# Half blocks of 128 rows for the experts' last rows, in both layers of a two-layer network

## The chip, the core and the metric

One core of a Trainium2 chip. The core has five engines that run their own queues of instructions and wait for each other by semaphores: TensorE (PE in the profile; PEld is its loading of weights), VectorE (DVE), ScalarE (ACT), GpSimdE (POOL) and SyncE (SP, which here only starts transfers). The metric is the device time of one execution in microseconds (us), lower is better; times of a kernel are medians over several executions.

## The reference

4096 tokens of 256 channels pass through two layers. Each layer normalizes the tokens and adds an attention part and a part of experts to them, both computed from the same normalized tokens. Layer 0 has a state-space mixer and 16 experts of width 128, of which a router gives 4 to each token (plus two shared ones that take every token); layer 1 has a linear attention and 8 experts of width 512, of which each token gets 2. First the experts of layer 0, then those of layer 1:

```python
scores = jax.nn.sigmoid(x @ w_gate.T)
...
_, idx = jax.lax.top_k(masked, TOPK)
w = jnp.take_along_axis(scores, idx, axis=1)
w = w / (w.sum(-1, keepdims=True) + 1e-06) * ROUTE_SCALE
...
g = jax.nn.silu(jnp.einsum('th,efh->tef', x, w1_e))
u = jnp.einsum('th,efh->tef', x, w3_e)
routed = jnp.einsum('tef,ehf,te->th', g * u, w2_e, combine)
...
topk_scores, topk_idx = jax.lax.top_k(scores, k)
topk_probs = jax.nn.softmax(topk_scores, axis=-1)
h1 = jnp.einsum('bsd,efd->bsef', x, W1)
h2 = jnp.einsum('bsd,efd->bsef', x, W2)
hidden = jax.nn.silu(h1) * h2
expert_out = jnp.einsum('bsef,edf->bsed', hidden, W3)
```

The kernel doesn't compute every expert for every token as the formulas do. It sends each token's row only to the experts that were chosen for it: 4096 x 4 = 16384 rows in layer 0, 4096 x 2 = 8192 in layer 1. How many rows an expert gets is known only while the kernel runs.

## The kernel before, in words

**Blocks.** The rows of an expert are laid out in DRAM (`xg0_d`, `xg1_d`) in blocks of `RB` = 256 rows, `RPB` = 2 tiles of 128. Every expert starts a new block, so its last block is mostly not full; what is empty holds zeros and the numbers of spare tokens (`blanks`, L318, called by `fills`, L1027). At most `NB0` = 79 and `NB1` = 39 blocks can be needed. The program runs `FIRST0` = 72 and `FIRST1` = 36 of them in any case, and the others only under a guard that compares the count of blocks, `used`, with that (L1134 and L1135, L1545). A block that no expert needs runs on blank rows.

**Routing.** `places` (L224 to L290) works on DVE, on all 128 partitions alike. It counts the rows of each expert (`plb`, a sum over token tiles), compares the counts with multiples of 256 (L260) and sums the comparisons to blocks per expert (`n_b`, L262), sums these along the experts by one small addition after the other (L264 to L267), and from that makes the place of each token's row (`dest`), the expert of each block (`own`, `owner`: a comparison of all blocks with all experts, L285 to L288) and `used`. It is a generator: at each `yield` other work is put between. In layer 0 three pieces of the routing go into each of the first steps of the mixer's main loop; in layer 1 one piece goes beside each step of the attention's projections (`beside`, L1296). Then each token's row is scattered by POOL to its places (`dispatch0`, L678, from step `FILLED` = 14 of the main loop on; L1274 in layer 1, two scatters a step).

**Layer 0's blocks.** The main loop of the mixer has 128 steps. When the dispatch is done, ticks of the blocks go into the remaining steps, two per step as long as there are more ticks left than steps, then one; there are `FIRST0` + 3 = 75 ticks, and consecutive blocks are in different stages of a tick: `block_in` (L727, 4 transposes), `block_hidden` (L742, 4 matmuls of 256 columns, two records each in the trace, L749), `block_out` (L759, 2 matmuls, L766) and `block_add` (L774, 2 indirect transfers by POOL that add the rows to `moe_d`, L779, each behind those of the block before). SP loads the block's rows, its expert's weights and the rows' shares (`block_rows`, `block_weights`). The orders of POOL and SP are written out by hand; those of PE, DVE and ACT come from the scheduler that builds the program.

**Layer 1's blocks** run at the end with nothing beside them. `some1` (L1525) goes through them with the next block's transposes and the block before's output between the two halves of the hidden layer: `load1` (L1436: the owner's number is read into a register of SP, then weights of 1 MB, rows, and 0.5 MB of output weights), `turn1` (L1449), `hidden1` (L1473, 16 matmuls of 256 columns, 32 records, L1482), `output1` (L1490, 8 matmuls, 16 records, L1496; then the scaling by the share on ACT, L1500, and two indirect adds to `out`, L1504). The weights of the hidden layer have two buffers, so those of a block are loaded when the block two before has read its own. The rows have two buffers as well.

Of the kernel before, what the change touches and what calls it, by code (L numbers as in the profile page):

```python
# [18 lines left out]
P = 128  # L19
# [31 lines left out]
NB0 = T * TOPK0 // RB + E0 - 1  # L51
NB1 = T * TOPK1 // RB + E1 - 1
FIRST0 = T * TOPK0 // RB + E0 // 2
FIRST1 = T * TOPK1 // RB + E1 // 2
# [48 lines left out]
def two_layer_kernel(  # L103
# [47 lines left out]

    xg0_d = dram.tile([NB0 * RB, RW0], FP, name="xg0_d")
    xg1_d = dram.tile([NB1 * RB, RW1], FP, name="xg1_d")
# [42 lines left out]

    def expert_of(owner, b, ne, behind=True):

        (ins,), (e,) = nc.values_load_multi_w_load_instructions(
            owner[0:1, b : b + 1], (mybir.EngineType.SP,), min_val=0, max_val=ne - 1,  # L200
            bass_reorder=False,
        )
        if loads and behind:
            tc.add_manual_dep(
                ins.ins, loads[-1].ins.name,
                mybir.DependencyInfo(mybir.DependencyClass.NoSync, mybir.DependencyReason.DATA),
                reason="in the order of the blocks",
            )
        return e
# [14 lines left out]
    def places(wk, psum, rk, ne, k, nb, dest, own, owner, used=None):  # L224

        t3 = lambda n: wk.tile([P, NT, ne], FP, tag="pl" + n, name="pl" + n, bufs=1)
# [31 lines left out]
        nc.vector.tensor_tensor(c3, last(a[:, NT - 1, :], steps), mid(full, ne), ALU.is_gt)  # L260
        n_b = wk.tile([P, ne], FP, tag="n_b", name="n_b", bufs=1)
        nc.vector.tensor_reduce(n_b, c3, AX.X, ALU.add)  # L262
        upb = wk.tile([P, ne], FP, tag="upb", name="upb", bufs=1)
        nc.vector.tensor_copy(upb[:, 0:1], n_b[:, 0:1])  # L264
        for e in range(1, ne):
            nc.vector.tensor_tensor(
                upb[:, e : e + 1], upb[:, e - 1 : e], n_b[:, e : e + 1], ALU.add  # L267
            )
        if used is not None:
            nc.vector.tensor_copy(used, upb[:, ne - 1 : ne])  # L270
# [3 lines left out]
        nc.vector.tensor_tensor(n_b, upb, n_b, ALU.subtract)  # L274
        nc.vector.tensor_scalar(n_b, n_b, float(RB), None, ALU.mult)
        nc.vector.tensor_tensor(a, a, mid(n_b, NT), ALU.add)
# [9 lines left out]
        nc.vector.tensor_reduce(own, cmp, AX.X, ALU.add)  # L286
# [26 lines left out]
    own0 = wpool.tile([P, NB0], FP, name="own0")  # L313
    owner0 = wpool.tile([P, NB0], I32, name="owner0")
# [3 lines left out]
    def blanks(xg, n, rw, b0, b1):  # L318
        v = xg.rearrange("(b j p) c -> p b j c", j=RPB, p=P)
        for j in range(RPB):  # L320
            nc.sync.dma_start(v[:, b0:b1, j, :], mid(blank[:, j, :rw], b1 - b0))
# [22 lines left out]
    with tc.tile_pool(name="m", bufs=1) as mp, tc.tile_pool(  # L344
# [333 lines left out]
        def dispatch0():  # L678

            def load(i):  # L680
                if i < NT:
                    xs = moe.tile([P, RPB * DM], FP, tag="ys", name=f"xs0_{i}", bufs=3)[:, :RW0]
                    o = i % TPB * P
                    nc.sync.dma_start(xs[:, :DM], xn_d[0][i // TPB][o : o + P, :])
                    ahead.append(xs)

            ahead = []
            load(0)
            yield
            for i in range(NT):  # L690
                load(i + 1)
                xs = ahead.pop(0)
                nc.gpsimd.tensor_copy(xs[:, DM:], tail0[:, i, :])
                for k in range(TOPK0):
                    nc.gpsimd.indirect_dma_start(
                        out=views0[i * TOPK0 + k],
                        out_offset=bass.IndirectOffsetOnAxis(ap=dest0[:, i, k : k + 1], axis=0),
                        in_=xs,
                        in_offset=None,
                        bounds_check=NB0 * RB - 1,  # L700
                    )
                    yield
# [3 lines left out]
        def block_rows(m):  # L706
            xg = moe.tile([P, RPB, RW], FP, tag="xg", name=f"xg0_{m}", bufs=2)
            nc.sync.dma_start(
                xg, xg0_d[m * RB : (m + 1) * RB, :RW].rearrange("(j p) c -> p j c", p=P)
            )  # L710
            rows0[m] = xg

        def block_weights(m):
            e = expert_of(owner0, m, E0, False)
# [6 lines left out]
                ws, xg0_d[m * RB : (m + 1) * RB, RW:]  # L721
# [5 lines left out]
        def block_in(m):  # L727

            xg = rows0.pop(m)
            pt = psum(f"ptx0_{m}").rearrange("p (k t) -> p k t", k=KD)  # L730
            for k in range(KD):
                for j in range(RPB):
                    nc.tensor.transpose(
                        pt[:, k, j * P : (j + 1) * P], xg[:, j, k * P : (k + 1) * P], ident
                    )
            xgt = moe.tile([P, KD, RB], FP, tag="xgt", name=f"xgt0_{m}", bufs=2)
            nc.scalar.copy(xgt, pt)
            ids = moe.tile([P, RPB], I32, tag="ids", name=f"ids0_{m}", bufs=5)
            nc.scalar.copy(ids, xg[:, :, DM])
            act0[m] = xgt, ids  # L740

        def block_hidden(m):  # L742
            xgt, ids = act0.pop(m)
            w, ws = weights0.pop(m)
            pgu = psum(f"pgu0_{m}").rearrange("p (a t) -> p a t", a=2)
            for a in range(2):
                for k in range(KD):
                    o = (a * KD + k) * P
                    nc.tensor.matmul(  # L749
                        pgu[:, a, :], w[:, o : o + P], xgt[:, k, :],  # L750
# [3 lines left out]
            nc.scalar.activation(sl, pgu[:, 0, :], AF.Silu)  # L754
            hid = moe.tile([P, RB], FP, tag="hid", name=f"hid0_{m}", bufs=2)
            nc.vector.tensor_tensor(hid, sl, pgu[:, 1, :], ALU.mult)
            hid0[m] = w, hid, ws, ids

        def block_out(m):  # L759
            w, hid, ws, ids = hid0.pop(m)  # L760
            po = psum(f"po0_{m}").rearrange("p (j d) -> p j d", j=RPB)
# [3 lines left out]
            for j in range(RPB):  # L765
# [4 lines left out]
            for j in range(RPB):  # L770
                nc.scalar.activation(ys[:, j, :], po[:, j, :], AF.Copy, scale=ws[:, j : j + 1])
            ys0[m] = ys, ids

        def block_add(m):  # L774
            ys, ids = ys0.pop(m)
            parts = []
            for j in range(RPB):
# [12 lines left out]

        def blocks(at):

            for m in range(FIRST0 + 3):
                if at == 0:
                    if m == 0:
                        block_rows(0)
                        block_rows(1)
                        block_weights(0)
                    if m < FIRST0:
                        block_in(m)  # L800
                if at == 1 and 0 <= m - 1 < FIRST0:
                    block_hidden(m - 1)
                if at == 3 and m >= 3:
                    block_add(m - 3)
                if at == 2:
                    if 0 <= m - 2 < FIRST0:
                        block_out(m - 2)
                    if m + 1 < FIRST0:
                        block_weights(m + 1)
                    if m + 2 < FIRST0:  # L810
                        block_rows(m + 2)
# [215 lines left out]
        def fills():  # L1027

            for b in range(0, NB0, 6):
                blanks(xg0_d, NB0, RW0, b, min(b + 6, NB0))  # L1030
# [7 lines left out]
            for b in range(0, NB1, 4):  # L1038
                blanks(xg1_d, NB1, RW1, b, min(b + 4, NB1))
# [5 lines left out]
        moe, sends, ticks, todo, done = None, None, None, FIRST0 + 3, object()  # L1045
# [88 lines left out]
        n0 = nc.values_load(used0[0:1, 0:1], min_val=T * TOPK0 // RB, max_val=NB0)  # L1134
# [108 lines left out]
    own = big.tile([P, NB1], FP, name="own")  # L1243
    owner = big.tile([P, NB1], I32, name="owner")
# [3 lines left out]
    def route1():  # L1248
# [15 lines left out]
        for g in range(NFB):  # L1264
# [6 lines left out]
            for j in range(TPB):  # L1271
                i = g * TPB + j
                for k in range(TOPK1):
# [5 lines left out]
                        bounds_check=NB1 * RB - 1,  # L1279
# [156 lines left out]
    def load1(b):  # L1436
# [3 lines left out]
        nc.sync.dma_start(w, wv_[:, : 2 * KD * fd])  # L1440
        xg = wk.tile([P, RPB, RW1], FP, tag="xs", name=f"xg{b}")
        loads.append(nc.sync.dma_start(
            xg, xg1_d[b * RB : (b + 1) * RB, :].rearrange("(j p) c -> p j c", p=P)
# [5 lines left out]
    def turn1(b):  # L1449
        w, xg, w2 = rows1.pop(b)  # L1450
        wt = wk.tile([P, RPB, E1], FP, tag="wt", name=f"wt{b}", bufs=4)
        tc.keep_in_program_order(nc.vector.scalar_tensor_tensor(
            wt, mid(lane[:, :E1], RPB), own[:, b : b + 1], xg[:, :, RW:], ALU.is_equal, ALU.mult
        ))
        ws = wk.tile([P, RPB], FP, tag="ws", name=f"ws{b}", bufs=4)
        nc.vector.tensor_reduce(ws, wt, AX.X, ALU.add)
        ids = wk.tile([P, RPB], I32, tag="ids", name=f"ids{b}", bufs=5)
        tc.keep_in_program_order(nc.vector.tensor_copy(ids, xg[:, :, DM]))
        pt = trp.tile([P, KD, RB], FP, tag="tr", name=f"ptx{b}")
        for k in range(KD):  # L1460
            for j in range(RPB):
# [6 lines left out]
        nc.scalar.copy(xgt, pt)  # L1468
# [4 lines left out]
    def hidden1(b, f0):  # L1473
        w, xgt, hid = act1[b]
        nm = f"1_{b}_{f0}"
        pg = ps.tile([P, 2, RB], FP, tag="pg", name="pg" + nm)
        pu = ps.tile([P, 2, RB], FP, tag="pu", name="pu" + nm)
        for a, pt in enumerate((pg, pu)):
            for f in range(2):
                for k in range(KD):  # L1480
                    o = (a * KD + k) * fd + (f0 + f) * P
                    nc.tensor.matmul(  # L1482
                        pt[:, f, :], w[:, o : o + P], xgt[:, k, :],
# [3 lines left out]
        nc.scalar.activation(sl, pg, AF.Silu)  # L1487
        nc.vector.tensor_tensor(hid[:, f0 : f0 + 2, :], sl, pu, ALU.mult)  # L1488

    def output1(b):  # L1490
        w2, hid, ws, ids = out1.pop(b)
        po = ps.tile([P, RPB, DM], FP, tag="po", name=f"po1_{b}")
        ys = wk.tile([P, RPB, DM], FP, tag="ys", name=f"ys{b}", bufs=4)
        for j in range(RPB):
# [7 lines left out]
        for j in range(RPB):  # L1502
# [15 lines left out]
    def count():  # L1518
# [3 lines left out]
        n = nc.values_load(now[0:1, 0:1], min_val=T * TOPK1 // RB, max_val=NB1)  # L1522
        counted.append(n)

    def some1(b0, b1):  # L1525
        load1(b0)
        turn1(b0)
        if b0 + 1 < b1:
            load1(b0 + 1)
        for b in range(b0, b1):  # L1530
# [3 lines left out]
            if b > b0:  # L1534
                output1(b - 1)
            if b + 1 < b1:
                turn1(b + 1)
            hidden1(b, 2)
            if b + 2 < b1:
                load1(b + 2)  # L1540
        output1(b1 - 1)


    some1(0, FIRST1)
    with tc.If(counted[0] > FIRST1):  # L1545
        some1(FIRST1, NB1)
# [65 lines left out]
```

## Time and profile before

| | us |
|---|---|
| median of 3 runs (lowest to highest) | 2320.83 (2318.41 to 2330.72) |
| the profiled execution: its time | 2315.34 |
| the profiled execution: its span, first to last instruction | 2313.6 |
| from the start to the end of the mixer with layer 0's experts beside it | about 0 to 1645 |
| of it: layer 0's routing pieces until `dest` is there | until 245 |
| of it: rows scattered to the blocks | 283 to 931 |
| of it: blocks of layer 0 | about 930 to 1630 |
| shared experts, attention and routing of layer 1 | about 1645 to 1912 |
| blocks of layer 1 | 1912 to 2313.6 |

A row of the profile names an engine, a line of the kernel, an operation with what it writes and reads, its partitions x elements, and how often it occurred; then its busy time, the mean of one in ns, and the idle time of the engine just before it, with what ended most of that. A matmul's time is the time from its start to its modelled end, and matmuls are pipelined: how far their starts are apart is read from the timeline, which merges like instructions into one line (start, length, engine, line, what, how many). The mean granted TensorE clock of the execution was 0.977 of the full one.

### The profile page before, as it was taken

How to read it: one execution, taken by the hardware profiler on the slowest of the kernel's cores; microseconds unless marked ns; L12 is line 12 of the kernel's file. 1: busy time of each engine (PE TensorE's matmuls, PEld its weight loads, DVE VectorE, ACT ScalarE, POOL GpSimd, SP SyncE). 2: the span in 40 equal slices, each digit the busy share in tenths (PEclk: the TensorE clock that was granted, in tenths of full speed). 3: DMA queues.
4: the chain of work that ended last, by engine and by line, in shares of the span. 5: the costliest groups of instructions: out<-in, count | busy, mean ns of one | idle time of the engine just before them, and what ended most of it. 6: DMA issues, size and time to landing. Idle time of an engine off the chain costs nothing. (4 is left out here: it accounts for less than half of the span.)

```text
span 2313.6 us, 36420 instructions
## 1 busy us (share of the span) xinstructions
PE 2143.8 (93%) x12572; PEld 1699.5 (73%) x12572; DVE 1455.9 (63%) x3350; ACT 910.0 (39%) x1872; POOL 1466.7 (63%) x1280
## 2 busy tenths in 40 slices
PE   6787999999999989899998999999799989999998
PEld 5565777777777767777787878888465568888886
DVE  5799988888888878556565567778257441111111
ACT  5632344343333334344443444444134742222221
POOL 0345699888889889677887787887541652232232
PEclk9899999999999999999999999999899999999999
DMA  9577678644444444576777776665541356777774
GB/s 312 172 217 230 187 239 256 193 142 155 146 135 159 146 137 145 166 186 174 180 183 179 181 183 162 172 173 150 175 136 46 131 191 182 207 187 197 202 190 113
DMA packets 240605, 405.72 MB, mean 175 GB/s; under 512 B 39201, under 2 KB 178977, under 8 KB 235809
## 3 DMA queue, kind: packets, MB, share of 16 engines
q1 hardware_dynamic: 193424, 342.62, 46.5%
q0 software_dynamic: 40320, 55.21, 13.5%
q10 hardware_dynamic: 6672, 5.51, 0.7%
q8 instruction: 103, 1.69, 0.3%
q14 instruction: 86, 0.70, 0.1%
HBM read 288.57 MB, written 114.69 MB: 174 GB/s over the span
## 5 line engine op out<-in xcount | busy, mean ns | idle before, releaser
L375 DVE SCALAR_TENSOR_TENSOR cv<-pj,cw,cv 128x256 f32<-128x256 f32 x864 | 404.1, 480 | 104.4 <-ACT cv L373 95.4
L519 POOL TENSOR_TENSOR mm<-mm,btok 128x512 f32<-128x512 f32 x256 | 336.9, 1397 | 13.6 <-DVE mm L470 12.8
L470 DVE TENSOR_TENSOR_SCAN mm<-mm,eyes 128x256 f32<-128x256 f32 x512 | 319.0, 672 | 24.4 <-ACT eyes L476 24.4
L365 PE MATMUL pj<-xt,w_in 128*128 128x259 f32 (+1 forms) x1152 | 314.4, 398 | 10.2 <-DVE pj L361 6.8
L435 PE MATMUL pg<-xt,w_in 128*128 128x256 f32 x1024 | 277.8, 393 | 35.0 <-ACT gate L442 32.3
L1504 POOL DMA_INDIRECT out<-ys,ids x72 | 111.3, 1546 | 300.2 <-ACT ys L1500 267.1
L365 PEld LDWEIGHTS pj<-xt,w_in 128*128 128x128 f32 x1152 | 217.7, 195 | 78.3 <-issue 34.7
L779 POOL DMA_INDIRECT moe_d<-ys,ids x144 | 226.8, 1575 | 69.4 <-issue 23.3
L597 PE MATMUL po<-w_o,g 128*128 128x256 f32 x1024 | 256.3, 383 | 1.8 <-POOL g L1021 1.8
L435 PEld LDWEIGHTS pg<-xt,w_in 128*128 128x128 f32 x1024 | 187.0, 194 | 92.5 <-ACT gate L442 42.4
L1488 DVE TENSOR_TENSOR hid<-silu,pu 128x512 f32<-128x512 f32 x72 | 49.5, 688 | 321.6 <-PE pu L1482 321.6
L373 ACT ACTIVATE cv<-pj,cw 128x256 f32<-128x256 f32 x288 | 135.7, 472 | 240.8 <-PE pj L365 239.6
L509 POOL TENSOR_TENSOR hd<-hdt,dec 128x512 f32<-128x512 f32 x124 | 140.9, 1137 | 117.0 <-DVE hdt L500 112.9
L597 PEld LDWEIGHTS po<-w_o,g 128*128 128x128 f32 x1024 | 190.4, 191 | 29.1 <-issue 2.7
L1021 POOL TENSOR_TENSOR g<-g,gate 128x512 f32<-128x512 f32 x128 | 176.2, 1377 | 51.2 <-DVE g L574 29.2
L386 ACT ACTIVATE hc<-cv,bw 128x256 f32<-128x256 f32 x256 | 129.5, 507 | 164.4 <-DVE cv L375 164.1
L574 DVE SCALAR_TENSOR_TENSOR g<-hc,ch,py 128x128 f32<-128x128 f32 x512 | 144.9, 344 | 27.2 <-PE py L563 27.0
L589 ACT ACTIVATE g<-g 128x512 f32<-128x512 f32 x128 | 80.8, 632 | 202.1 <-POOL g L593 146.2
L474 DVE TENSOR_TENSOR cs<-cs,eyes 128x512 f32<-128x512 f32 x248 | 159.9, 675 | 0.0
L563 PE MATMUL py<-cs,state 128*64 128x128 f32 x1984 | 144.0, 284 | 14.2 <-issue 10.9
L563 PEld LDWEIGHTS py<-cs,state 128*64 128x64 f32 x1984 | 110.0, 139 | 59.5 <-issue 53.7
L749 PE MATMUL pgu<-xgt,w 128*128 128x256 f32 x576 | 142.8, 393 | 11.2 <-DVE state L545 11.1
(245 smaller groups left out, 3999.7 us busy)
## 6 DMA issues: line engine op xcount, KB each, us to landing
mm<-step_d SPq DMA_DIRECT2D x128, 512.0 KB, 4.5
cs<-from_d SPq DMA_DIRECT2D x124, 512.0 KB, 5.9
w<-in_w_ffn SPq DMA_DIRECT2D x36, 1024.0 KB, 5.7
w<-in_w_ffn SPq DMA_DIRECT2D x72, 384.0 KB, 3.2
xg_d<-blank SPq DMA_DIRECT2D x26, 828.0 KB, 8.4
xg<-xg_d SPq DMA_DIRECT2D x72, 260.0 KB, 4.1
w<-in_w_ffn SPq DMA_DIRECT2D x36, 512.0 KB, 6.5
xg_d<-blank SPq DMA_DIRECT2D x18, 536.0 KB, 8.4
```

The lines of the kernel that those rows point to most:

```text
L365: nc.tensor.matmul(pj[:, h0 : TB + HALO], w_in[:, k, INTER + c * P : INTER + (c + 1) * P], xts[b][:, k, h0 : TB + HALO], start=(k == 0), s ...
L375: nc.vector.scalar_tensor_tensor(cv, pj[:, i : i + TB], cw[:, c, i : i + 1], cv, ALU.mult, ALU.add)
L435: nc.tensor.matmul(pj[:, :TB], w_in[:, k, c * P : (c + 1) * P], xts[b][:, k, HALO:], start=(k == 0), stop=(k == KD - 1),)
L470: nc.vector.tensor_tensor_scan(m, m, eye, 0.0, ALU.mult, ALU.add)
L474: nc.vector.tensor_tensor(m, m, mid(c_in[:, j, :], QH), ALU.mult)
L519: nc.gpsimd.tensor_tensor(m, m, mid(blk["gm"][j], QH), ALU.mult)
L563: nc.tensor.matmul(py[(h % 2) * HP : (h % 2 + 1) * HP, h // 2, :], left[:, h, :], right[:, h, :], start=(a == 0 and h < 2), stop=(a == len ...
L574: nc.vector.scalar_tensor_tensor(g[:, i, :], hc[i][:, sl], d_ch[:, k : k + 1], py[:, i, :], ALU.mult, ALU.add,)
L597: nc.tensor.matmul(po[:, j, :], g[:, i, :], w_o[:, k, :], start=(k == 0 and j == 0), stop=(k == NCI - 1), skip_group_check=True,)
L749: nc.tensor.matmul(pgu[:, a, :], w[:, o : o + P], xgt[:, k, :], start=(k == 0), stop=(k == KD - 1),)
L779: nc.gpsimd.indirect_dma_start(out=moe_d[:, :], out_offset=bass.IndirectOffsetOnAxis(ap=ids[:, j : j + 1], axis=0), in_=ys[:, j, :], in_of ...
L1021: nc.gpsimd.tensor_tensor(gs[k], gs[k], gates[n][:, :, j * P : (j + 1) * P], ALU.mult)
```

## The change

Both layers get blocks of two sizes. An expert whose rows, counted modulo 256, leave a rest of 1 to 128 gives this rest to a half block of 128 rows instead of a whole block. There are 8 half blocks in layer 0 and 4 in layer 1 (`NH0`, `NH1`); if more experts have such a rest, the further ones take a whole block as before. The half blocks lie behind the whole ones in DRAM (`place`), and the program runs 64 and 32 whole blocks (`FIRST0`, `FIRST1`) and all half blocks unguarded, in the order of `mixed`: one half after every eight whole ones. The number of blocks that run stays 72 and 36. At most `NB0` = 71 and `NB1` = 35 whole blocks can be needed; those above 64 and 32 run under the guard, which compares with the count of whole blocks. In `places` a second comparison with the multiples of 256 plus 128 tells experts with such a rest from the others, two scans make the running sums in place of the chain of additions, rows of the rest get another place, the half blocks get their owners, and one more `yield` stands in it. Every operation of a block works on `nj` tiles of 128 rows, 2 or 1; the weights are loaded whole for each.

```diff
+def most(n, ne, nh):
+    return max(
+        (n - h - (ne - h) * (RB // 2 + 1)) // RB + ne - h + max(h - nh, 0) for h in range(ne + 1)
+    )
+
+NH0, NH1 = E0 // 2, E1 // 2
+NB0, NB1 = most(T * TOPK0, E0, NH0), most(T * TOPK1, E1, NH1)
+FIRST0, FIRST1 = T * TOPK0 // RB, T * TOPK1 // RB
...
+    def place(b, nb):
+        return (b * RB, RPB) if b < nb else (nb * RB + (b - nb) * P, 1)
+
+    def mixed(first, nb, nh):
+        n = first // nh
+        return [b for h in range(nh) for b in (*range(h * n, (h + 1) * n), nb + h)]
...
-        nc.vector.tensor_tensor(c3, last(a[:, NT - 1, :], steps), mid(full, ne), ALU.is_gt)
+        nc.vector.tensor_tensor(c3, last(n_e, steps), mid(full, ne), ALU.is_gt)
+        nc.vector.tensor_reduce(odd, c3, AX.X, ALU.add)
+        nc.vector.tensor_scalar_add(full, full, float(P))
+        nc.vector.tensor_tensor(c3, last(n_e, steps), mid(full, ne), ALU.is_gt)
         nc.vector.tensor_reduce(n_b, c3, AX.X, ALU.add)
-        nc.vector.tensor_copy(upb[:, 0:1], n_b[:, 0:1])
-        for e in range(1, ne):
-            nc.vector.tensor_tensor(
-                upb[:, e : e + 1], upb[:, e - 1 : e], n_b[:, e : e + 1], ALU.add
-            )
...
+        nc.vector.tensor_tensor(odd, odd, n_b, ALU.subtract)
+        nc.vector.tensor_tensor_scan(upo, ones[:, :ne], odd, 0.0, ALU.mult, ALU.add)
+        nc.vector.scalar_tensor_tensor(odd, upo, float(nh), odd, ALU.is_gt, ALU.mult)
+        nc.vector.tensor_tensor(n_b, n_b, odd, ALU.add)
+        nc.vector.tensor_tensor_scan(upb, ones[:, :ne], n_b, 0.0, ALU.mult, ALU.add)
+        nc.vector.tensor_copy(used, upb[:, ne - 1 : ne])
 
         yield
         nc.vector.tensor_tensor(a, a, w, ALU.add)
-        nc.vector.tensor_tensor(n_b, upb, n_b, ALU.subtract)
+        first, extra = s1("first"), s1("extra")
+        nc.vector.tensor_tensor(first, upb, n_b, ALU.subtract)
+        nc.vector.tensor_scalar(first, first, float(RB), None, ALU.mult)
+        nc.vector.tensor_scalar(
+            extra, upo, float(P), float(nb * RB - P), ALU.mult, ALU.add
+        )
+        nc.vector.scalar_tensor_tensor(extra, upb, -float(RB), extra, ALU.mult, ALU.add)
         nc.vector.tensor_scalar(n_b, n_b, float(RB), None, ALU.mult)
-        nc.vector.tensor_tensor(a, a, mid(n_b, NT), ALU.add)
+        nc.vector.tensor_tensor(b, a, mid(n_b, NT), ALU.is_ge)
+        nc.vector.tensor_tensor(b, b, mid(extra, NT), ALU.mult)
+        yield
+        nc.vector.tensor_tensor(a, a, mid(first, NT), ALU.add)
+        nc.vector.tensor_tensor(a, a, b, ALU.add)
         yield
...
-        nc.vector.tensor_reduce(own, cmp, AX.X, ALU.add)
+        nc.vector.tensor_reduce(own[:, :nb], cmp, AX.X, ALU.add)
+        nc.vector.tensor_tensor(cmp[:, :nh, :], mid(upo, nh), last(thr[:, :nh], ne), ALU.is_le)
+        nc.vector.tensor_reduce(own[:, nb:], cmp[:, :nh, :], AX.X, ALU.add)
...
         def block_hidden(m):
...
+            n = place(m, NB0)[1] * P
...
-                        pgu[:, a, :], w[:, o : o + P], xgt[:, k, :],
+                        pgu[:, a, :n], w[:, o : o + P], xgt[:, k, :n],
...
         def block_add(m):
...
-            for j in range(RPB):
+            for j in range(place(m, NB0)[1]):
...
+        order0 = mixed(FIRST0, NB0, NH0)
...
-            for m in range(FIRST0 + 3):
+            for m in range(len(order0) + 3):
...
-            for b in range(0, NB0, 6):
-                blanks(xg0_d, NB0, RW0, b, min(b + 6, NB0))
+            n = NB0 + NH0 // RPB
+            for b in range(0, n, 6):
+                blanks(xg0_d, RW0, b, min(b + 6, n))
...
     def hidden1(b, f0):
...
+        n = place(b, NB1)[1] * P
...
-                        pt[:, f, :], w[:, o : o + P], xgt[:, k, :],
+                        pt[:, f, :n], w[:, o : o + P], xgt[:, k, :n],
...
-    some1(0, FIRST1)
+    some1(mixed(FIRST1, NB1, NH1))
     with tc.If(counted[0] > FIRST1):
-        some1(FIRST1, NB1)
+        some1(range(FIRST1, NB1))
```

`block_in`, `block_out`, `turn1`, `output1` and the loads of rows and shares are cut to `nj` tiles in the same way.

## The prediction

> **What bounds the kernel now.** I read the page's busy shares first, then the windows by stage.
>
> ```profile
> PE 2143.8 (93%) x12572; PEld 1699.5 (73%) x12572; DVE 1455.9 (63%) x3350; ACT 910.0 (39%) x1872; POOL 1466.7 (63%) x1280
> ```
> ```profile
> 200.00:250.00 50.00, 35.32 (x224) 27.05 (x222) 50.00 (x112) 15.14 (x28) 23.73 (x21) 0.86 0.53 164
> 300.00:930.00 630.00, 590.27 (x4058) 464.11 (x4058) 541.26 (x1191) 244.49 (x520) 557.78 (x527) 0.99 0.53 167
> 930.00:1390.00 460.00, 434.72 (x2677) 353.04 (x2674) 272.36 (x581) 201.25 (x496) 355.02 (x270) 0.97 0.71 179
> 1390.00:1630.00 240.00, 237.63 (x1637) 198.05 (x1637) 187.07 (x395) 110.20 (x253) 195.34 (x154) 1.00 0.61 159
> 1950.00:2250.00 300.00, 300.00 (x1447) 262.77 (x1446) 49.52 (x140) 74.98 (x139) 85.24 (x56) 1.00 0.73 197
> ```
> After the stretch and its length come the busy times of PE, PEld, DVE, ACT and POOL, then granted clock, DMA share and GB/s. Routing of layer 0 (200 to 250) fills DVE. Layer 0's blocks run beside the mixer (930 to 1390 two blocks a step, to 1630 one): PE is busy 95% and 99%. Layer 1's blocks (1950 to 2250) keep PE busy without a gap. So in both places that the change touches, PE work is the time.
>
> One block of layer 1 in the timeline:
>
> ```profile
> 2004.96 0.38 SPq L1442 DMA_DIRECT2D xg<-xg_d  x1
> ...
> 2007.36 1.89 PE L1482 MATMUL pg<-xgt,w 128*128 128x256 f32 x8
> 2007.56 0.33 SPq L1440 DMA_DIRECT2D w<-in_w_ffn  x1
> ...
> 2009.09 1.89 PE L1482 MATMUL pu<-xgt,w 128*128 128x256 f32 x8
> 2010.82 1.89 PE L1496 MATMUL po<-w,hid 128*128 128x256 f32 x8
> ...
> 2015.13 0.60 PE L1462 MATMUL ptx<-ident,xg 128*128 128x128 f32 x4
> ...
> 2018.16 1.89 PE L1482 MATMUL pg<-xgt,w 128*128 128x256 f32 x8
> ```
> Eight records start every 1.73 us: 0.216 us for one at 256 columns. A block is 32 of them for the hidden layer, 16 for the output, 4 transposes (0.135 each: 0.54); the same row returns after 10.80 us.
>
> **How many blocks run.** I worked the reference's router out on its inputs. Layer 0's experts get 1082, 1113, 1003, 1070, 1015, 1040, 978, 930, 1015, 1030, 987, 1023, 973, 1043, 1050, 1032 rows; layer 1's 992, 1005, 851, 1553, 1054, 1082, 767, 888. Rounded up to 256 that is 72 and 36 blocks, exactly FIRST0 and FIRST1. Eight experts of layer 0 end in 1 to 128 rows, five of layer 1, for eight and four halves. So the changed kernel needs 64 whole + 8 half and 32 whole + 4 half, again exactly what runs unguarded. The page bears out that no tail ran before (2x72 and 2x36):
>
> ```profile
> L1504 POOL DMA_INDIRECT out<-ys,ids x72 | 111.3, 1546 | 300.2 <-ACT ys L1500 267.1
> ...
> L779 POOL DMA_INDIRECT moe_d<-ys,ids x144 | 226.8, 1575 | 69.4 <-issue 23.3
> ```
> Twelve blocks become halves; nothing else is dropped, and each half still loads its whole weights.
>
> **A matmul of 128 columns.** The blocks have none behind 128-column weights except transposes. The nearest row is the product of attention's values, same type, same weights:
>
> ```profile
> 1799.37 1.86 PEld L1362 LDWEIGHTS pvv<-vt 128*128 128x128 f32 x16
> 1799.46 1.96 PE L1362 MATMUL pvv<-vt 128*128 128x128 f32 x16
> ```
> Sixteen weight loads in 1.86 us: 0.116 each. The bounds: 0.108 (half of 0.216) and 0.190 (one load's own duration, L1482, if nothing overlapped). I take 0.116. [...]
>
> **Layer 1, 4 halves.** 32 x (0.216 - 0.116) = 3.2; 8 output records fewer, 1.73; 2 transposes fewer, 0.27: 5.2 us each, 15.6 for the three in the middle. What might eat it is the weights. L1440 is issued just after the block two before it has read its buffer (2007.56) and lands 5.1 to 6.7 us later; the reader starts 10.6 us after the issue, less if the block between is a half: 32 x 0.116 + 3.46 + 0.54 = 7.7 from the buffer's release, so 0.7 to 2 us remain. One block on, L1440 stands on SP behind the row load and the owner's read (2.60 us, 2004.96 to 2007.56): issued about 2.9 us behind the transposes, landing by 9.6 at worst, wanted after some 10.4. Scatters leave 4.1 us between start and landing; output to output is never under 6.9 us in the middle. So I cost these at nothing; without that slack the two readers behind a half could lose about 1 us each.
>
> The last half ends the kernel. Now:
>
> ```profile
> 2296.86 1.55 POOL L1504 DMA_INDIRECT out<-ys,ids  x1 [1.05 <-ACT ys L1500]
> ...
> 2301.43 1.54 POOL L1504 DMA_INDIRECT out<-ys,ids  x1 [3.02 <-ACT ys L1500]
> ...
> 2303.99 1.55 POOL L1504 DMA_INDIRECT out<-ys,ids  x1 [1.01 <-ACT ys L1500]
> ```
> From 2296.86 to the last landing is 7.1 + 4 = 11 us. With one scatter, which must wait for the landing of the block before, it is 4 + 4 = 8: 3 saved. Ahead of it 16 records x 0.1, 2 transposes, 0.1 more: 2.0. Layer 1: 15.6 + 5.0 = 20.6 us; bounds 11 (loads at 0.190, weights late) and 22.
>
> **Layer 0, 8 halves.** 8 records of L749 x 0.1, 2 of L766 x 0.216, 2 transposes of L733 x 0.135: 1.5 us of PE, 12 in all. POOL loses a scatter of 1.58 and its gap of 0.3 in each; ACT and DVE less work too, so no other engine is made later. Steps and ticks stay 75. Bounds: 0, if the 5% idle of PE shows that chains set these steps, and 15, if POOL does. I take 12, by the windows.
>
> **Routing.** In layer 0 it is DVE's time:
>
> ```profile
> L266 DVE TENSOR_TENSOR upb<-upb,n_b 128x1 f32<-128x1 f32 x15 | 5.8, 387 | 0.0
> ...
> L276 DVE TENSOR_TENSOR plb<-plb,n_b 128x512 f32<-128x512 f32 x1 | 0.7, 681 | 0.0
> L260 DVE TENSOR_TENSOR plc<-plb,full 128x256 f32<-128x256 f32 x1 | 0.4, 414 | 0.0
> ```
> The fifteen additions and a copy go (5.9). Added: a second comparison and its sum (0.82), three passes over 128x512 (2.04), nine on 16 columns (0.16 each, 1.4; two are scans, which the trace has only at 256 columns, 0.67: 0.16 to 0.67 each), the halves' owners (0.5), less 0.4 for the shorter owner table: 4.4. Small ones also stretch (0.15 to 0.79 in L266), so the net is -3 to +2; I take -0.5. The extra yield moves routing's end from step 11 to 12; scatters start at step 14 regardless. In layer 1 the same grows by some 2 us, beside projections that PE sets; it also delays the scatters one step, perhaps 2 us, and the first row load (1896.4, landing by 1903 at the longest), wanted only at 1912: 9 us of cover. The blank fills shrink by four blocks and by two.
>
> The built order moves DVE's scans and products among neighbours in 300 to 930 and PE's pieces little. PE idles 40 us there (630.0 - 590.3); I guess a tenth of that either way, 4 us, and take 0.
>
> **Sum.** 20.6 + 12 + 0.5 = 33 us. The profiled execution took 2315.3 (span 2313.6): 2282. The median of the runs is 2320.8, 5.5 above it: **2288**.
>
> **The rivals.**
> *Weight loads set the spacing* (0.190): a middle half saves 2.8, the last 3.8, layer 0's 0.9 each: 12.2 + 7.2 + 0.5 = 20, 2301. For it: PEld is busy 88% in layer 1. Against: L1362. [...] Chance 0.07.
> *Weights come late behind halves in layer 1*: 3 halves x 2 readers x up to 2 us, 12 back: 2300. For: slack under 2 us. Against: L1440 never took over 6.7. The granted clock was 1.00 in this stage. [...] Chance 0.07.
> *Chains, not PE, set layer 0's steps*: 12 lost, 2300. For: PE waits on DVE's state at L749. Against: 95 to 99% busy. Chance 0.08.
> *A tail runs*, the slower side. The guards at L1135 and L1545 have no row of margin: if one whole block above 64 or 32 is needed, because rounding moves two tokens to the expert of 1023 or 767, all the tail's blocks run. Layer 1: 3 blocks x 10.8, plus unhidden loads (2.6 + 5.7) and a landing (4): 45. Layer 0: 7 blocks in a row, each at least two scatters (3.8) and a wait for the landing (about 3): 50. So 2288 + 47 = 2335. Against: such a move would also have run the tails before. Chance 0.04.
>
> **How the numbers follow.** The forecast holds 0.74. Its own range: -5 (POOL sets layer 0, routing -3) to +9 (PE's waits stay, order): 2281 to 2297. The three milder rivals reach 2304 with the runs' scatter: range **2279 to 2306**. A change within 0.5%, 11.6 us, can't be told from none. Faster: all but the tail and a sum of two mild rivals: 0.92; same 0.04; slower 0.04.
>
> **What would show it.** Scatters 136 and 68; hidden records of 128 columns starting 0.116 us apart; whole blocks still 10.8 us apart in layer 1 and halves 5.6; no PE wait for weights behind a half; layer 1's stage 20 us shorter, 930 to 1630 shorter by 12. More scatters mean a tail, and the prediction falls; if 300 to 930 moves by over 5 us, the order mattered.

## The result and the profile after

The changed kernel took 2294.7 us (median of 4 runs, 2293.07 to 2298.88), the kernel before on the same chip 2323.57 us (median of 4, 2318.41 to 2330.72). The ratio is 0.9878, 95% interval 0.9857 to 0.99: 28 us less, 23 to 33. The forecast was 2288, the range 2279 to 2306. The profiled execution took 2293.07 us, its span 2291.3.

The page's busy times and its groups of scatters:

```profile
PE 2117.2 (92%) x12500; PEld 1681.3 (73%) x12500; DVE 1456.1 (64%) x3358; ACT 896.5 (39%) x1860; POOL 1446.7 (63%) x1268
```
```profile
L1555 POOL DMA_INDIRECT out<-ys,ids x68 | 105.2, 1547 | 286.0 <-ACT ys L1551 179.3
...
L820 POOL DMA_INDIRECT moe_d<-ys,ids x136 | 214.0, 1573 | 84.4 <-issue 25.2
```

68 and 136 scatters, four and eight fewer than before: twelve blocks became halves and no tail ran. PE lost 26.6 us of busy time; whether that time stood on the path is another matter. The windows by stage, with the columns of the prediction:

```profile
200.00:250.00 50.00, 35.87 (x222) 29.06 (x223) 50.00 (x110) 14.70 (x28) 25.04 (x21) 0.83 0.49 153
300.00:930.00 630.00, 591.94 (x4040) 466.27 (x4039) 538.98 (x1186) 242.67 (x520) 554.40 (x526) 0.98 0.53 165
930.00:1390.00 460.00, 427.16 (x2639) 346.57 (x2638) 269.04 (x574) 195.32 (x486) 344.54 (x265) 0.96 0.71 174
1390.00:1630.00 240.00, 236.58 (x1640) 197.45 (x1639) 189.23 (x399) 110.24 (x256) 193.45 (x154) 1.00 0.63 161
1950.00:2250.00 300.00, 300.00 (x1489) 264.45 (x1488) 49.60 (x145) 75.08 (x144) 86.51 (x56) 1.00 0.75 203
```

Layer 1's stage is full of PE work, as before. Between 930 and 1390, where two blocks of layer 0 stand in most steps of the mixer, PE is busy 427.16 us where it was 434.72: the halves' work is gone, but the stage is not shorter, PE idles more in it.

Layer 1, around its first half block in the timeline of the changed kernel (start, duration, then what ran):

```profile
1981.54 0.60 PE L1511 MATMUL ptx<-ident,xg 128*128 128x128 f32 x4
...
1992.34 0.38 PE L1511 MATMUL ptx<-ident,xg 128*128 128x128 f32 x2
1992.56 1.03 PE L1532 MATMUL pg<-xgt,w 128*128 128x256 f32 x4
1993.43 1.89 PE L1532 MATMUL pu<-xgt,w 128*128 128x256 f32 x8
1995.15 1.05 PE L1532 MATMUL pg<-xgt,w 128*128 128x128 f32 x8
1996.04 1.06 PE L1532 MATMUL pu<-xgt,w 128*128 128x128 f32 x8
1996.94 1.89 PE L1547 MATMUL po<-w,hid 128*128 128x256 f32 x8
...
2001.22 0.60 PE L1511 MATMUL ptx<-ident,xg 128*128 128x128 f32 x4
...
2007.96 0.60 PE L1511 MATMUL ptx<-ident,xg 128*128 128x128 f32 x4
...
2019.62 0.60 PE L1511 MATMUL ptx<-ident,xg 128*128 128x128 f32 x4
```

Eight records at 128 columns start 0.89 us before the next eight: 0.111 each. From the transposes at 1981.54 to those at 2019.62, four blocks further, are 38.08 us; four whole blocks take 4 x 10.80 = 43.20. So this half saved 5.1 us. The saving is spread over three distances because the next block's transposes stand inside the block. PE waits for nothing between 1915 and the end: the view of its waits is empty there.

From layer 1's first transposes to the end of the span were 401.4 us (1912.24 to 2313.6) and are 380.3 (1911.05 to 2291.3): 21.1 saved. The mixer with layer 0's blocks ends where it did: the last matmul of its output projection (`po<-w_o,g`) starts at 1642.1 in the profile of before and at 1641.9 in this one. So between these two executions, whose spans differ by 22.3 us, nearly the whole gain is layer 1's. The medians of the runs differ by more, and the experiments ask what layer 0 gave.

### The profile page after: what moved, and what is told of

Same layout as the page of the kernel before. It is cut to its first block, busy times and chain, and to the rows that moved or that the text cites. A ratio compares the mean times of both kernels' runs of the same rounds, so it can differ in the third digit from the quotient of the medians.

```text
span 2291.3 us, 36246 instructions
## 1 busy us (share of the span) xinstructions
PE 2117.2 (92%) x12500; PEld 1681.3 (73%) x12500; DVE 1456.1 (64%) x3358; ACT 896.5 (39%) x1860; POOL 1446.7 (63%) x1268
## 4 chain that ended last, share of the span: by engine, by line
PE 57%; POOL 17%; DVE 10%; issue 6%; ACT 4%; DMA 4%; SPq 1%; ACTq 0%; POOLq 0%; DVEq 0%
PE pj L400 6%; PE py L598 5%; PE pg L1532 5%; PE pu L1532 5%; PE po L1547 5%; PE pgu L789 5%; PE po L632 5%; PE pg L470 4%; POOL mm L554 4%; POOL xg_d L730 3%; POOL state L574 3%; PE pb L1355 2%; PE po L807 2%; POOL g L628 2%; PE pst L567 2%
## 5 line engine op out<-in xcount | busy, mean ns | idle before, releaser
L400 PE MATMUL pj<-xt,w_in 128*128 128x259 f32 (+1 forms) x1152 | 319.6, 404 | 9.2 <-DVE pj L396 6.6
L1555 POOL DMA_INDIRECT out<-ys,ids x68 | 105.2, 1547 | 286.0 <-ACT ys L1551 179.3
L820 POOL DMA_INDIRECT moe_d<-ys,ids x136 | 214.0, 1573 | 84.4 <-issue 25.2
L1538 DVE TENSOR_TENSOR hid<-silu,pu 128x512 f32<-128x512 f32 (+1 forms) x72 | 47.4, 658 | 304.9 <-PE pu L1532 304.9
L789 PE MATMUL pgu<-xgt,w 128*128 128x256 f32 (+1 forms) x576 | 138.3, 386 | 17.9 <-DVE state L580 17.9
```

Source lines behind the costliest of these rows:

```text
L400: nc.tensor.matmul(pj[:, h0 : TB + HALO], w_in[:, k, INTER + c * P : INTER + (c + 1) * P], xts[b][:, k, h0 : TB + HALO], start=(k == 0), s ...
L789: nc.tensor.matmul(pgu[:, a, :n], w[:, o : o + P], xgt[:, k, :n], start=(k == 0), stop=(k == KD - 1),)
L820: nc.gpsimd.indirect_dma_start(out=moe_d[:, :], out_offset=bass.IndirectOffsetOnAxis(ap=ids[:, j : j + 1], axis=0), in_=ys[:, j, :], in_of ...
```

## The experiments

Twelve kernels ran in three groups (e1 to e4, e5 to e8, e9 to e12), each group on a chip of its own. A ratio is to the kernel before, which ran beside each group: 2322.98 us in the first, 2361.6 and 2357.63 in the others. A saving in us against the kernel before is worked out from the ratio in the first two groups and from the medians in the third; two other kernels are compared by their medians. In the second and third group every kernel is slower between the layers. That stretch in the changed kernel:

```profile
1790.00:1960.00 170.00, 160.45 (x693) 115.46 (x692) 66.81 (x166) 85.88 (x134) 78.43 (x92) 0.98 0.52 167
```

and in the same kernel run again in the second group:

```profile
1790.00:1960.00 170.00, 132.60 (x529) 89.42 (x528) 58.58 (x138) 75.79 (x114) 68.50 (x86) 0.88 0.38 130
```

PE is busy 28 us less in the same 170, and the granted clock is 0.88 where it was 0.98; why is not shown. So times are compared within a group, and stages by their own marks. One mark is the state's matmul (`pst`), by which the steps are counted here. It comes once a step, but for the last three counts, which hold two steps each. Steps 80 to 123 hold nearly all of layer 0's blocks, and their length is taken from the timeline as the distance of the start of step 79's `pst` from step 123's. It is 689.6 us in the profile of before and 690.4 in that of the change.

### One layer alone

e1 has halves in layer 1 alone, e2 in layer 0 alone; the other layer's routing, block count and order are those of before.

```diff
-NH0, NH1 = E0 // 2, E1 // 2
+NH0, NH1 = 0, E1 // 2          # e1;  e2: E0 // 2, 0
```

> Half blocks in layer 1 alone; layer 0 keeps its 72 whole blocks and its old routing. If a half's saving is TensorE's work with nothing given back, the last stage is 20.6 us shorter and the ratio to before is about 0.991 (2323.6 - 20.6 = 2303). If weights arrive late behind halves, it is 8 to 12 us (0.995).

> Half blocks in layer 0 alone. If TensorE's work sets the mixer's steps, 12 us less: ratio 0.995. If chains through other engines set them (the two profiles so far end the mixer at 1641.8 and 1641.7), 0 to 3 us: ratio 0.999 to 1.000.

e1: 2305.13 us, ratio 0.9917 (0.9897 to 0.9938), 19 us. Its layer 1 took 381.2 us from the first transposes to the end (1927.22 to 2308.4), 20.2 less than before. e2: 2311.64 us, ratio 0.9944 (0.9922 to 0.9967), 13 us (8 to 18). The two together make 32 us, as far as the intervals tell the change's 28. Yet e2's profile shows steps 80 to 123 at 689.0 us, no shorter than before's. And e1, whose PE, POOL, ACT and DVE run the same instructions in the same order there as before's, shows 701.1. So executions of one and the same code differ there by 11 us, and one profile can't size layer 0's gain; the profile of before was at the lower end (2315.3 us, the runs 2318 to 2332).

### Layer 0: PE's work or POOL's scatters

A half saves PE 1.5 us by the forecast, and POOL one of the two indirect adds. e3 keeps PE's, ACT's and DVE's whole work and the loads for 256 rows, and saves the scatter alone. e4 saves the work and keeps the second scatter, to 128 spare rows that nobody reads. Both have layer 1 as before.

```diff
 # e3: block_rows, block_weights, block_in, block_hidden, block_out
-nj = place(m, NB0)[1]
+nj = RPB
 # e4: block_add
-for j in range(place(m, NB0)[1]):
+half = place(m, NB0)[1] == 1
+for j in range(RPB):
...
-ap=ids[:, j : j + 1]
+ap=(spare if half and j else ids[:, j : j + 1])
...
-in_=ys[:, j, :]
+in_=ys[:, 0 if half else j, :]
```

> Layer 0's half blocks load, transpose and multiply 256 rows as whole ones do (the second 128 rows are those of the next place and are dropped), and only their scatter is a half's: one indirect add instead of two. If TensorE's work is on the path in layer 0, nothing is gained: ratio 1.000. If GpSimd's queue sets the steps, it gains what layer 0's halves gain as they are.

> Layer 0's half blocks have a half's work on TensorE, ScalarE and VectorE, but two indirect adds as a whole block has; the second adds the same rows to 128 more spare tokens. If TensorE's work is on the path: ratio 0.995 as with the halves as they are. If GpSimd's queue sets the steps: 1.000.

e3: 2317.09 us, ratio 0.9974 (0.9961 to 0.9987), 6 us. e4: 2321.34 us, ratio 0.9999 (0.9984 to 1.0013): nothing. PE's saving alone is worth nothing, the scatter's alone 6 us, both 13. In single profiles steps 80 to 123 took 690.8 us in e3 and 694.9 in e4, which the 11 us of the same code cover. PE's work is there to be saved: in steps that nothing disturbs, e4 is as short as the change (step 85: 14.9 us before, 14.2 in both). It is given back in others. What takes it is a wait of PE for the mixer's state, which the view of PE's waits between 935 and 1415 us shows (us in all, times, the longest). Before:

```profile
PE pgu L749 <- DVE state L545: 11.1, 6, 3.5
```

and in e4:

```profile
PE pgu L859 <- DVE state L650: 22.9, 14, 6.3
```

In e3 it is 9.7 us in 7, in the change 17.9 in 7. One of the change's in the timeline, POOL first:

```profile
1097.60 1.57 POOL L820 DMA_INDIRECT moe_d<-ys,ids  x1 [0.87 <-DMA moe_d<-ys,ids]
1099.47 1.58 POOL L820 DMA_INDIRECT moe_d<-ys,ids  x1 [0.30 <-issue]
1100.50 1.63 POOL L574 TENSOR_TENSOR state<-state,dec 128x512 f32<-128x512 f32 x1
1101.50 3.07 POOL L554 TENSOR_TENSOR mm<-mm,btok 128x512 f32<-128x512 f32 x2
```

then DVE and PE in the same microseconds:

```profile
1102.16 0.69 DVE L580 TENSOR_TENSOR state<-state,pst 128x512 f32<-128x512 f32 x1 [3.29 <-POOL state L574]
```
```profile
1096.52 1.13 PE L567 MATMUL pst<-hd,btok 128*128 128x512 f32 x2
1097.48 1.04 PE L400 MATMUL pj<-xt,w_in 128*128 128x259 f32 x4
1098.36 0.60 PE L772 MATMUL ptx<-ident,xg 128*128 128x128 f32 x4
1098.79 1.03 PE L470 MATMUL pg<-xt,w_in 128*128 128x256 f32 x4
1102.91 3.78 PE L789 MATMUL pgu<-xgt,w 128*128 128x256 f32 x8 [3.09 <-DVE state L580]
1106.48 1.93 PE L400 MATMUL pj<-xt,w_in 128*128 128x259 f32 x4
```

Read from the top: in a step with two blocks the second `block_add` comes last on POOL. Its adds waited for the landing of the block before, and the next step's state product (L574) stands behind them. DVE's addition of the state (L580) waits for that product, and only this addition frees the buffer of `pst`. `pst`, `ptx` and `pgu` share two buffers of PSUM, so PE's `pgu` waits 3.09 us. Behind the wait the same eight matmuls take 3.78 us instead of 1.89 and `pj` 1.93 instead of 1.04. The clock has been halved: the window's granted clock, the third number from the end, is 0.52.

```profile
1102.00:1109.00 7.00, 6.09 (x17) 4.86 (x18) 2.52 (x6) 0.86 (x2) 5.35 (x5) 0.52 0.42 72
```

So this wait of 3.09 us costs about 6: `pgu` loses another 1.9 us and `pj` 0.9.

### Taking the scatters away from the state product

e8 is the changed kernel again, for the second group. In e5 and e6 (the change, and the kernel before) the second `block_add` is issued earlier in the step. In e7 it keeps its place, but the next step's state product is issued ahead of it, into a tile of its own; `block_hidden` multiplies in place to make room.

```diff
 # e5, e6
+            if t > 1:
+                next(ticks[3])
             out_ = project(*half[k - 3], gs.pop(k - 3)) if k >= 3 else iter(())
...
-            if t > 1:
-                next(ticks[3])
 # e7: carry() is the POOL half of advance()
             if t > 1:
+                if k + 1 < len(half):
+                    carry(*half[k + 1])
                 next(ticks[3])
```

> The changed kernel; only the second block_add of a step with two blocks is issued on POOL earlier: after the step's inputs (hd) instead of at its end, so that the next step's state product no longer stands behind it. PE's order is unchanged. Theory (POOL's scatters at the end of a two-block step delay the state product, PE waits about 3 us for the state, and then runs at half rate for a while): the PE waits 'pgu<-DVE state' between 935 and 1415 us fall from 17.9 us in 7 to under 6, and the time is 5 to 12 us under that of the unmoved kernel run beside it (about 2283 to 2290). Rival (PE's own work is the time there and the waits are only moved): within 3 us of the unmoved kernel. Second rival (POOL's sum of work per step is the limit, so the order of its items is indifferent, and the scatter now holds the sq sum and the output): same or slower by up to 8 us.

> The same move in the kernel before the change. Theory: the kernel before has more such steps with four scatters each, so it gains at least as much as the changed one, 5 to 12 us against the kernel before (ratio 0.995 to 0.998), and the halves' worth on top of it is then PE's and POOL's work alone. Rival (PE's work is the time): ratio 0.999 to 1.001. Rival (POOL's sum of work): 1.000 to 1.004.

> The changed kernel; in a step with two blocks the next step's state product (POOL) is issued ahead of the second block_add, into a tile of its own, and block_hidden multiplies in place to make room for it. The scatters keep their places otherwise. Theory: the waits for the state go as in the run with the earlier add, 5 to 12 us faster than the unmoved kernel; if this one gains and the earlier add does not, it was the state product and not the place of the scatter. Rival (PE's work): within 3 us.

> The changed kernel unchanged, for an interval on the same chip and a second profile. Both theories: ratio 0.986 to 0.990 to the kernel before; the stage of layer 0 with the mixer ends within 12 us of the first profile (its waits for the state are not the same ones in each execution), layer 1's stage 379 us within 1 us.

e8: 2325.29 us, ratio 0.9841 (0.9822 to 0.9859), 38 us here. Its layer 1 took 380.4 us, as in the first profile (380.3). Steps 80 to 123 took 682.6 where the first had 690.4.

e5: 2336.35 us, ratio 0.9898 (0.9884 to 0.9913), 11 us slower than e8. e6: 2370.79 us, ratio 1.0039 (1.0022 to 1.0057). The expected gain fell: both moves made a new wait. e5's POOL in the timeline:

```profile
1094.35 1.56 POOL L820 DMA_INDIRECT moe_d<-ys,ids  x1 [0.31 <-issue]
1096.22 1.58 POOL L820 DMA_INDIRECT moe_d<-ys,ids  x1 [0.30 <-issue]
1097.72 1.16 POOL L544 TENSOR_TENSOR hd<-hdt,dec 128x512 f32<-128x512 f32 x1
1102.25 1.57 POOL L820 DMA_INDIRECT moe_d<-ys,ids  x1 [3.37 <-ACT silu L794]
1104.12 1.58 POOL L820 DMA_INDIRECT moe_d<-ys,ids  x1 [0.30 <-PE py L598]
1105.13 1.87 POOL L628 TENSOR_TENSOR g<-g,g 128x512 f32<-128x512 f32 x1
```

and ACT's, which wrote the two tiles of `ys` that the adds at 1102.25 and 1104.12 send:

```profile
1097.27 0.84 ACT L812 ACTIVATE ys<-po,ws 128x256 f32<-128x256 f32 x2 [1.79 <-PE po L807]
```

The view names ACT's `silu` as what ended the wait of 3.37 us, because a `silu` ended just before the add. But the data had been there for 4 us. What the add also needs is the landing of the adds that it follows. By the trace's semaphore events the one from 1096.22 landed at 1101.48, and the add started 0.77 us later; behind a landing that the view does name the distance is the same (0.74 us for the add at 1097.60 in the change). Between 935 and 1415 us POOL waited over 0.45 us before an add 26 times in e5. In 24 of these, 57.7 us in all, the add starts 0.73 to 0.83 us behind such a landing; in e8 it is 38.3 us in 25. No add in that stretch of e5 starts less than 1.8 us behind its `ys`, though the view puts 36.9 us of its waits down to ACT's `silu` and `ys`. So the second block's adds now stand at POOL's head while the first block's are still on their way, and all that follows on POOL waits with them. PE's `pgu` waited 17.3 us for the state, where e8 below shows 13.1. e6 is the same: 67.1 us of such waits in 31, where the kernel before has 37.1 in 25.

e7: 2308.46 us, ratio 0.9776 (0.9756 to 0.9797), 53 us under the kernel before and 17 under e8. By its ratio it is the fastest version of all; on this chip the change itself took 2325. PE's waits in e8 between 935 and 1415 us (us in all, times, the longest):

```profile
PE pgu L789 <- DVE state L580: 13.1, 8, 2.8
PE psq L648 <- DVE state L580: 6.2, 3, 3.3
...
PE pst L567 <- POOL hd L544: 1.8, 1, 1.8
```

and in e7:

```profile
PE pst L586 <- POOL hd L544: 8.1, 6, 2.8
...
PE psq L661 <- DVE state L593: 1.1, 2, 0.8
```

The waits for the state are gone from `pgu`, and nearly from `psq`. Another has grown: PE's `pst` waits for POOL's `hd`, now the first product behind the adds. Steps 80 to 123 took 666.4 us, 16.2 less than in e8: as far as one profile of each can tell, nearly the whole gain lies there.

### The halves again, with the state first

Is PE's work the time once that wait is gone? e9 is the kernel before with the state product first (into `hd`'s two buffers). e10, e11 and e12 are e2, e4 and e3 with the same edit, so e9 is their base.

> The kernel before (no halves); the next step's state product on POOL is issued ahead of the second block_add of a step with two blocks, into a tile that shares hd's two buffers. Theory (scatters ahead of the state product make PE wait, and the clock falls behind the wait): as in the changed kernel, 12 to 20 us faster than the kernel before (ratio 0.991 to 0.995). Rival (the state product was late only with the halves' order of work): ratio 0.998 to 1.001.

> State product first, and half blocks in layer 0 alone (layer 1 as before). To be compared with the kernel without halves run beside it that has the state product first. Both theories: 9 to 14 us less than that one.

> As the run before it in this call (state product first, halves in layer 0 alone), but each half makes two indirect adds, the second to spare rows: PE's saving without POOL's. Without the state product first this was worth 0 us. Theory (PE's work is the time once PE no longer waits for the state): 6 to 12 us less than the kernel with the state product first and no halves. Rival (POOL's scatters set the steps in any case): within 3 us of it.

> State product first, halves in layer 0 alone do the whole work of a block on every engine but make one indirect add: POOL's saving without PE's. Without the state product first this was worth 6 us. Theory (PE's work is the time once PE no longer waits for the state): 0 to 3 us less than the kernel with the state product first and no halves. Rival (POOL's scatters set the steps in any case): 6 to 12 us less.

| kernel | median, us | ratio to before (95%) | steps 80-123, us | PE's `pst` waits for `hd`, us (times) |
|---|---|---|---|---|
| e9, no halves | 2336.53 | 0.9914 (0.9896-0.9932) | 670.8 | 3.6 (2) |
| e10, halves | 2330.42 | 0.9883 (0.986-0.9906) | 664.7 | 6.0 (5) |
| e11, work halved, two scatters | 2339.99 | 0.9934 (0.9909-0.996) | 674.6 | 15.4 (9) |
| e12, whole work, one scatter | 2333.91 | 0.9894 (0.9876-0.9912) | 670.4 | 2.9 (2) |

The edit is worth 21 us without any halves (e9): the old order cost the kernel before about as much as it cost the change. But neither theory fits all three kernels with halves. e11 is not 6 to 12 us under e9, as it should be if PE's work were the time; its median is 3.5 over it. e12 is under it by 2.6, not by the 6 to 12 that would follow if the scatters alone set the steps. e10 is under it by 6, not 9 to 14. The intervals of e10, e11 and e12 all overlap that of e9, so only the order of size can be read. The steps of the single profiles agree with it, but their differences are within the 11 us that the same code showed above: against e9, e10 shortens steps by 10.3 us in all and lengthens others by 4.3; e11 shortens by 7.5 and lengthens by 11.3. Where e11's time goes is its last column, and POOL shows why:

```profile
1102.92 1.57 POOL L904 DMA_INDIRECT moe_d<-ys,ids  x1 [0.56 <-ACT ids L861]
1104.80 1.58 POOL L904 DMA_INDIRECT moe_d<-ys,spare  x1 [0.30 <-issue]
...
1112.93 1.56 POOL L904 DMA_INDIRECT moe_d<-ys,ids  x1 [3.26 <-DMA moe_d<-ys,spare]
1114.79 1.58 POOL L904 DMA_INDIRECT moe_d<-ys,ids  x1 [0.30 <-issue]
1115.82 3.07 POOL L624 TENSOR_TENSOR mm<-mm,btok 128x512 f32<-128x512 f32 x2
1118.28 1.83 POOL L1150 TENSOR_TENSOR g<-g,gate 128x512 f32<-128x512 f32 x1
1121.09 1.56 POOL L904 DMA_INDIRECT moe_d<-ys,ids  x1 [0.98 <-ACT ids L861]
1122.96 1.58 POOL L904 DMA_INDIRECT moe_d<-ys,ids  x1 [0.30 <-issue]
1123.99 1.63 POOL L614 TENSOR_TENSOR hd<-hdt,dec 128x512 f32<-128x512 f32 x1
1124.99 1.85 POOL L711 TENSOR_TENSOR g<-g,g 128x512 f32<-128x512 f32 x1
1126.22 1.62 POOL L637 TENSOR_TENSOR scaled<-state,dec 128x512 f32<-128x512 f32 x1
```

From the adds at 1112.93 to the end of the state product at 1127.84 one round of POOL takes 14.9 us, of which 0.98 is a wait. An undisturbed step with two whole blocks takes 14.9 us on PE (e9, step 105), one with a half 14.2 (step 85 above). So POOL's round, 13.9 us without a wait, is nearly as full as PE's, and it also waits for landings: the add at 1104.80 had not landed when the next could have gone at about 1109.7, and 3.26 us were lost. A shorter step for PE with the same POOL round only makes PE wait. That two rounds of nearly equal length are why e10 gains only 6 us is argued from this round, not shown: the runs vary the scatters and PE's work apart, but not the landings.

## Why the prediction was right, and where it was not

- **Layer 1, 20.6 us: right.** 21.1 between the profiles, 20.2 in e1's, 19 by e1's ratio. A middle half saved 5.1 us (5.2 forecast), the records came 0.111 us apart (0.116 taken), and the weights were never waited for. The last indirect add starts at 2282.86 us where it started at 2303.99. "5.6 us apart" was ill put: a half's saving shows in three distances.
- **Weight loads set the spacing (2301): refuted** by the 0.111 us: halving the columns from 256 to 128 halved the distance of the records here, from 0.216 to 0.111 us.
- **Weights late behind halves (2300): refuted**; PE waits for nothing in that stage.
- **Layer 0, 12 us: the size held, its ground did not.** e2 measured 13 us (8 to 18); the change less e1 leaves 9, e8 less layer 1's 21 leaves 17. That the number held is luck. "PE work is the time", read from windows at 95% and 99%, failed: PE's work alone gave 0 us (e4) and nothing with the state first (e11), the scatter alone gave 6 (e3). The step that failed is "POOL loses a scatter ... so no other engine is made later", which priced the scatters at nothing. They stand on the path, in POOL's queue ahead of the state product. The scatter's saving is worth 6 us by itself, PE's only together with it.
- **Chains, not PE, set layer 0's steps (2300): half right.** Its sign in the profile (PE's waits for DVE's state) was the true one. It left out that a half's missing scatter also shortens the chain (e3).
- **The granted clock: 1.00 in layer 1, before and after**, and PE of the changed kernel waited for nothing there. In layer 0 the forecast had nothing for the clock, and it cost time: behind the wait of 3.09 us it was 0.52 in a window of 7 us, and eight matmuls of `pgu` took 3.78 us, not 1.89 (more in the last section).
- **Routing, -0.5 us, and the order, 0: too small to matter, if not exact.** Step 79 starts at 931.4 us before and 932.3 after, far under the 5 us that would have counted. In the four kernels without halves in layer 0 it starts at 928.5 to 931.4, in the ten with them at 930.4 to 935.0, 2 us later in the mean.
- **930 to 1630 shorter by 12: not seen** (689.6 and 690.4 us for steps 80 to 123). As a sign it was unfit: identical code differs there by 11 us between executions.
- **No tail**: 136 and 68 scatters.
- **The sum**: 33 us forecast, 28 measured (23 to 33), 38 in the second group (33 to 42).

## What to carry to other kernels

A window in which PE is busy 95% does not make PE's work the time: ask what stands in the queue of each engine that PE waits for, add up a whole round of that engine, and read PE's few waits as the sign. When a change shortens work on two engines of nearly equal rounds, cost them together; either alone may be worth nothing. Issue the product that the next step's critical engine needs ahead of a scatter that may wait for a landing, and keep a scatter well behind the one whose landing it must wait for. Where a view names what ended a wait, compare it with the times at which the data were written and the transfers landed.

## What the runs showed of the hardware

- **Matmuls behind a wait of PE could be slower, but not behind every one.** In the profiles of before, the change, e4, e5, e6 and e8 `pgu` waits for the state 59 times between 930 and 1420 us. No wait under 1.9 us was followed by slower matmuls. The shortest that was is 1.91 us (e8: eight matmuls in 3.17 us, not 1.99). The longest that was not is 2.81 (e8), and every one from 3.0 us up was. So it is not the gap's length alone.
- **Ahead of a halved clock PE's idle time and that of `psq` made 2.04 us or more together.** In the profiles of before and the change the granted clock is 1 or 0.5, and all its changes lie whole multiples of 3.41 us apart. Cut by these, there are 400 stretches of 3.41 us at full clock between 925 and 1640 us; 12 of them were followed by half the clock, for 3.41 or 6.83 us. In each of the 12, PE's idle time and the time of `psq`, matmuls of a single column (sixteen of them take 1.84 to 1.95 us), made 2.04 us or more together; of the 388 others one reached that, with 2.12, and the next has 1.98. Idle time alone does not part them: five of the 12 had 1.57 us or less of it, each beside `psq`, and one of the 388 had 1.95.
- **The same code in the mixer with layer 0's blocks took 689.6 and 701.1 us in two executions** (before and e1), and 690.4 and 682.6 in two of the changed kernel (e8 the second). In the first pair single steps differ by up to 4 us (step 92: 20.7 and 24.7) and undisturbed ones by under 0.1.
- **One order of two POOL instructions was worth more than the halves in layer 0**: 21 us in the kernel before (e9) against 13 (e2).
